# A perceiver layer on one core: the order of a program's branch arms, and the last products, sums and stores in halves

## The chip, the cores and the metric

The kernel runs on one core of a Trainium2 chip. The metric is the device time of the program in microseconds. Before the change three runs gave 994.02, 991.90 and 992.71, a median of 992.71. One more execution was recorded by the profiler; it took 989.35 us, and from its first to its last instruction 987.6 us.

TensorE (PE) multiplies, VectorE (DVE) and ScalarE (ACT) work on its results, GpSimd (POOL) computes and issues gathers, and SyncE (SP) issues most DMAs. Each engine has its own stream of instructions and its own sequencer, which handles waits, branches and the issue of DMAs. When a program branches, every engine has to branch.

## The reference

The input `x` is [1, 256, 512], the context [1, 4096, 512], all in float32. One layer is computed:

- cross attention of 256 queries with 16 heads of 128 (4 heads for keys and values) over the 4096 context rows and the layer's own rows (these causally), with RMS norm and rotary positions on queries and keys;
- a state-space block (projection, causal convolution, scan in chunks of 128, gate, projection);
- a mixture of experts. With `xn` the normalized state of a row:

```python
scores = sigmoid(xn @ gate_w)                 # 32 experts
w, e   = top_k(scores, 6); w = w / (sum(w) + 1e-20)
routed = sum_k w[k] * (silu(xn @ wg[e[k]]) * (xn @ wu[e[k]])) @ wd[e[k]]
shared = (silu(xn @ sg) * (xn @ su)) @ sd
out    = x + routed + shared
```

An expert's hidden size is 192, that of the shared expert 384. Each stage adds to the residual state, which the kernel keeps in `x_sb`, two tiles of 128 rows by 512 columns; what `x_sb` holds at the end is the output.

## The kernel before, in words

**Two branches.** Whether attention may use a fixed bound on its scores is computed from the norm weights on the chip (`small_scores`, line 110) and loaded into a register of every engine as `flag` (line 1601). At line 1602 the program branches: one arm is `layer(lctx, True)`, with bounded attention, the other (line 1605) is `layer(lctx, False)`. Both arms are written out in full. The data given take the bounded arm. The second branch stands near the end of the layer, at line 1572: `crowded` says whether some expert got more rows than its place holds, and is loaded as `some` (line 1557). The data given take the arm without crowding. It holds the last additions and the stores; the other arm runs all experts over again and comes after it in the program. At the end of the arm of line 1572 that is written first, an engine jumps over the code that follows: the crowded arm and the general layer.

**The experts.** Experts are worked on in 16 pairs (`NP`), one a round `n`. A round does the gate and up products (`gate_up`, or `gate_up_halves` where an expert of the pair has room for 64 rows), turns the hidden values, and does the down product of the round before. Rows come from `xg` by gather; results go to `ye` by a store on ACT's queue, and are gathered again by row (`gather`, line 1322, six rows per token, on POOL) and added with their weights on DVE (`add`, line 1330). The last three pairs (`n` from `LAST` = 13) don't pass through `ye`: `spread_last` brings their hidden values to token order with a product (lines 1424 and 1425) and `down_into` (line 1457) sums their down products for both row tiles in two PSUM banks, `total[0]` and `total[1]`. A float32 product is two passes of TensorE, each with its own weight load, so `down_into` of one tile has three products and six passes.

**The order at the end.** In the last round, `n` = 15, TensorE does `down_into` of pair 14 for tile 0, the spreading of pair 15, and `down_into` of pair 14 for tile 1; between them DVE adds the gathered rows of tile 1. After the loop `down_into` of pair 15 follows, tile 0 and then tile 1. In the arm without crowding, `finish(t)` (line 1567) adds `total[t]` to `x_sb` on DVE and `store(t)` (line 1570) issues the store on SP, once for each tile.

**Buffers touched.** `ps_x` is a pool of two PSUM banks with the tag `x`, used for the transposes of gathered rows (line 1370); the last of these belongs to pair 15. `total` comes from `ps_ye`.

**What closes the program.** After the joins, every engine comes to the program's end, which the profile puts down to line 1650: SP waits for the semaphores of all queues and engines, every engine drains and signals, and all meet twice. At the start, SP issues the first loads (lines 94 to 104) ahead of its branch and those of `wk`, `wq` and `wv` (line 189) behind it; TensorE's first product (line 218) stands behind the branch.

## Time and profile before

| | us |
|---|---|
| median of three runs (lowest, highest) | 992.71 (991.90, 994.02) |
| the profiled execution | 989.35 |
| its span, first to last instruction | 987.6 |
| TensorE busy | 968.4 |
| DVE busy | 497.8 |
| ACT busy | 386.5 |
| POOL busy | 206.0 |
| TensorE busy in the first 25 us | 19.60 |
| end of TensorE's last pass, by the chain | 979.71 |
| last addition on DVE, start and length | 979.74, 0.69 |
| the two stores, start of issue | 977.95, 980.46 |

"Busy" counts the instructions of an engine's datapath, not branches, waits or the issue of DMAs. The chain of work that ended last is followed back from the last such instruction, so what comes after it has no part in it. A line that ends in q (SPq, DVEq, PEldq) is of an engine's sequencer. In the list for one source line, a row gives the operation, how often it ran, its least, median and greatest duration in ns, and the start of the first and of the last one in us. The queues called "instruction" bring instructions to the engines.

### The profile page before, as it was taken

How to read it: one execution, taken by the hardware profiler on the slowest of the kernel's cores; microseconds unless marked ns; L12 is line 12 of the kernel's file. 1: busy time of each engine (PE TensorE's matmuls, PEld its weight loads, DVE VectorE, ACT ScalarE, POOL GpSimd, SP SyncE). 2: the span in 40 equal slices, each digit the busy share in tenths (PEclk: the TensorE clock that was granted, in tenths of full speed). 3: DMA queues.
4: the chain of work that ended last, by engine and by line, in shares of the span. 5: the costliest groups of instructions: out<-in, count | busy, mean ns of one | idle time of the engine just before them, and what ended most of it. 6: DMA issues, size and time to landing. Idle time of an engine off the chain costs nothing.

```text
span 987.6 us, 8901 instructions
## 1 busy us (share of the span) xinstructions
PE 968.4 (98%) x2742; PEld 456.0 (46%) x2742; DVE 497.8 (50%) x999; ACT 386.5 (39%) x851; POOL 206.0 (21%) x212
## 2 busy tenths in 40 slices
PE   7999999999999999999999999999999999999996
PEld 3444444444444444444444444444465655555442
DVE  4456555454453544544535545458496766422134
ACT  3645444443443434434434444353253731222210
POOL 4443001001100200200200100000013224554533
PEclk9999999999999999999999999999999999999999
DMA  9734142222313304304204112240046452999953
GB/s 319 235 74 118 56 117 94 45 39 111 85 21 128 85 2 147 82 4 150 66 20 124 56 35 46 83 128 1 0 157 199 184 193 106 353 351 352 397 221 117
DMA packets 131580, 125.91 MB, mean 127 GB/s; under 512 B 80225, under 2 KB 99586, under 8 KB 126274
## 3 DMA queue, kind: packets, MB, share of 16 engines
q1 hardware_dynamic: 119216, 77.96, 26.2%
q0 software_dynamic: 7984, 41.16, 11.2%
q10 hardware_dynamic: 4322, 6.11, 1.7%
q8 instruction: 24, 0.39, 0.2%
q14 instruction: 34, 0.28, 0.1%
HBM read 89.02 MB, written 36.19 MB: 127 GB/s over the span
## 4 chain that ended last, share of the span: by engine, by line
PE 94%; DMA 2%; DVE 1%; ACT 1%; POOL 1%; issue 1%; SPq 0%; POOLq 0%; DVEq 0%
PE scT L567 23%; PE oT L592 23%; PE ps_kv L364 17%; PE ps_egu L218 5%; PE ps_self L218 3%; PE ps_v L218 2%; PE ps_o L790 2%; PE ps_ye L1466 2%; PE ps_xbc L218 1%; PE ps_out L984 1%; PE ps_egu L1389 1%; PE ps_k L218 1%; PE ps_sgu L218 1%; PE total L1457 1%; PE xgTp L1370 1%; PE ps_ye L1469 1%
## 5 line engine op out<-in xcount | busy, mean ns | idle before, releaser
L583 DVE TENSOR_TENSOR lacc<-lacc,prT 128x512 f32<-128x512 f32 x256 | 182.6, 714 | 239.2 <-ACT prT L573 238.5
L573 ACT ACTIVATE prT<-scT,bq,rk 128x512 f32<-128x512 f32 x256 | 198.9, 777 | 253.9 <-PE scT L567 241.8
L567 PE MATMUL scT<-qT,kT 128*128 128x512 f32 x536 | 271.7, 593 | 0.0
L592 PE MATMUL oT<-prT,v 128*128 128x512 f32 x528 | 268.3, 592 | 0.0
L567 PEld LDWEIGHTS scT<-qT,kT 128*128 128x128 f32 x536 | 101.1, 190 | 124.8 <-issue 121.9
L592 PEld LDWEIGHTS oT<-prT,v 128*128 128x128 f32 x528 | 100.2, 190 | 125.8 <-issue 115.8
L196 POOL TENSOR_TENSOR rk<-pv,mhalf 128x4 f32<-128x4 f32 x32 | 32.3, 1010 | 369.2 <-DVE pv L195 369.2
L364 PE MATMUL ps_kv<-wkv,fast 128*128 128x512 f32 x112 | 53.4, 592 | 0.0
L254 ACT ACTIVATE sq<-kraw 128x128 f32<-128x128 f32 x128 | 35.6, 278 | 45.2 <-DVE kraw L382 43.2
L364 PE MATMUL ps_kv<-wkv,ctx 128*128 128x512 f32 x112 | 52.8, 592 | 0.0
L364 PE MATMUL ps_kv<-fast,fast 128*128 128x512 f32 x112 | 52.6, 592 | 0.0
L598 DVE TENSOR_TENSOR oacc<-oT,oacc 128x512 f32<-128x512 f32 x64 | 43.6, 681 | 0.0
L364 PEld LDWEIGHTS ps_kv<-wkv,fast 128*128 128x128 f32 x112 | 21.3, 190 | 26.8 <-issue 26.8
L364 PEld LDWEIGHTS ps_kv<-fast,fast 128*128 128x128 f32 x112 | 21.3, 190 | 26.8 <-issue 21.8
L364 PEld LDWEIGHTS ps_kv<-wkv,ctx 128*128 128x128 f32 x112 | 21.3, 190 | 26.8 <-issue 23.7
L358 POOL TENSOR_TENSOR fast<-ctx 128x512 f32<-128x512 f32 x7 | 9.4, 1337 | 113.1 <-PE ps_kv L364 94.2
L382 DVE TENSOR_TENSOR kraw<-ps_kv,fast 128x256 f32<-128x256 f32 x42 | 17.9, 426 | 28.2 <-PE ps_kv L364 28.2
L1441 DVE TENSOR_TENSOR hid<-si,ps_egu 128x128 f32<-128x128 f32 x18 | 5.2, 287 | 51.2 <-ACT si L1439 51.2
L790 PE MATMUL ps_o<-wo,qT 128*128 128x512 f32 x64 | 28.8, 592 | 0.0
L218 PE MATMUL ps_self<-wq,xT 128*128 128x512 f32 x64 | 28.1, 592 | 0.0
L603 DVE RECIPROCAL lacc<-ps_l 128x512 f32<-128x512 f32 x8 | 26.8, 3348 | 0.1
L364 PE MATMUL ps_kv<-fast,ctx 128*128 128x512 f32 x56 | 26.3, 592 | 0.0
(392 smaller groups left out, 1129.3 us busy)
## 6 DMA issues: line engine op xcount, KB each, us to landing
xg<-xn SPq DMA_DIRECT2D x6, 2560.0 KB, 9.7
ctx<-in_ctxT_dram SPq DMA_DIRECT2D x7, 1024.0 KB, 5.0
kd<-tr SPq DMA_DIRECT2D x112, 64.0 KB, 2.2
kT<-kd SPq DMA_DIRECT2D x28, 256.0 KB, 2.9
ye<-y_sb ACTq DMA_DIRECT2D x22, 256.0 KB, 8.4
wq<-in_wq_dram SPq DMA_DIRECT2D x4, 1024.0 KB, 14.2
wo<-in_wo_dram SPq DMA_DIRECT2D x4, 1024.0 KB, 7.7
w_in<-in_W_inT_dram SPq DMA_DIRECT2D x4, 1024.0 KB, 5.8
```

The costliest lines, as they stand in the source:

```text
L196: return G.tensor_tensor(dst, v[:, :n], mhalf[:, :n], ALU.pow)
L218: TE.matmul(ps, lhs(k), rhs_of(k), start=(k == 0), stop=(k == KD - 1))
L254: S.activation(sq[:, h, :], raw[:, h, :], AF.Square, accum_out=ss[:, h:h + 1])
L364: TE.matmul(ps, lhs(k), rhs(k), start=(start and k == 0), stop=(k == 1), skip_group_check=True)
L567: scored.append(TE.matmul(sc, kT[:, g, i * P:(i + 1) * P], qT[:, t, heads4(g), :].rearrange("p h q -> p (h q)"), start=True, stop=True).ins)
L573: S.activation(pr, sc, AF.Exp, bias=shift, scale=SCALE if r is None else r[:, i, g:g + 1])
L583: V.tensor_tensor(la, la, pr, ALU.add)
L592: TE.matmul(outs[g, t], v[:, i, g * HD:(g + 1) * HD], pr, start=(n == 0), stop=last)
L598: V.tensor_tensor(ov, outs.pop((g, t)), ov, ALU.add)
L603: V.reciprocal(rl, ps)
L790: TE.matmul(m["ps_o", t], aT[:, t, h, :], wo[j][:, h % 4, :], start=(h == 0), stop=(h == NH - 1))
L1466: TE.matmul(ps[i], h[:, i, :], wd[i], start=True, stop=False)
```

## The change

There are four edits.

1. The arms of both branches change places: the test becomes `some == 1` with the crowded arm first, and `flag == 0` with the general layer first. The arms that the given data take are now the last in the program.
2. The additions `finish` move in front of the branch on `crowded`, out of both arms. In the common arm only stores are left.
3. `total[1]` no longer takes in pair 15: its sum ends with pair 14 and is added to `x_sb` at once. The product of pair 15 for tile 1 is done in two halves of 256 columns, each in a bank of its own from `ps_x` (`part`), and each half is added by itself.
4. The store of tile 1 is issued in two halves of columns.

```diff
-            def down_into(self, n, total, first, last, tiles=range(NT)):
+            def down_into(self, n, total, first, last, tiles=range(NT), cols=slice(0, DM)):
...
-                        TE.matmul(total[t], h[:, j, t * P:(t + 1) * P], wd[j],
+                        TE.matmul(total[t], h[:, j, t * P:(t + 1) * P], wd[j][:, cols],
...
-                        main.down_into(n - 1, total, False, False, [1])
+                        main.down_into(n - 1, total, False, True, [1])
...
-            main.down_into(NP - 1, total, False, True)
-
-            def finish(t):
-                V.tensor_tensor(x_sb[:, t, :], total[t], x_sb[:, t, :], ALU.add)
-
-            def store(t):
-                nc.sync.dma_start(out[t * P:(t + 1) * P, :], x_sb[:, t, :])
-
-            with tc.If(some == 0) as arms:
-                for t in range(NT):
-                    finish(t)
-                    store(t)
-            with arms.Else():
-                for t in range(NT):
-                    finish(t)
+            halves = [slice(i * DM // 2, (i + 1) * DM // 2) for i in range(2)]
+            parts = [main.ps_x.tile([P, DM // 2], FP, tag="x", name="part") for _ in halves]
+
+            def finish(t, ps, cols=slice(0, DM)):
+                V.tensor_tensor(x_sb[:, t, cols], ps, x_sb[:, t, cols], ALU.add)
+
+            def store(t, cols=slice(0, DM)):
+                nc.sync.dma_start(out[t * P:(t + 1) * P, cols], x_sb[:, t, cols])
+
+            main.down_into(NP - 1, total, False, True, [0])
+            finish(1, total[1])
+            for cols, part in zip(halves, parts):
+                main.down_into(NP - 1, {1: part}, True, True, [1], cols)
+            finish(0, total[0])
+            for cols, part in zip(halves, parts):
+                finish(1, part, cols)
+
+            with tc.If(some == 1) as arms:
                 main.weights = {}
...
                     store(t)
+            with arms.Else():
+                store(0)
+                for cols in halves:
+                    store(1, cols)
...
-    with tc.If(flag == 1) as arms:
+
+    with tc.If(flag == 0) as arms:
+        with ExitStack() as lctx:
+            layer(lctx, False)
+    with arms.Else():
         with ExitStack() as lctx:
             layer(lctx, True)
-    with arms.Else():
-        with ExitStack() as lctx:
-            layer(lctx, False)
```

## The prediction

> **What bounds the kernel now.** I read the page first, then the end of the chain that ended last, then the two lines of code at which the program branches and joins, then the DMAs of the last 9 us, then the start.

> ```profile
> PE 968.4 (98%) x2742; PEld 456.0 (46%) x2742; DVE 497.8 (50%) x999; ACT 386.5 (39%) x851; POOL 206.0 (21%) x212
> ```

> TensorE is busy for 98% of the span, so only the places where it isn't can give much. The windowed view shows 19.60 us of TensorE work in the first 25.00 us and none in 980 to 988. The chain's last pieces (start, length, what):

> ```profile
> 971.97 7.74 PE total L1457 x18
> 979.71 0.02 issue
> 979.74 0.69 DVE x_sb L1567
> ```

> The arithmetic is over at 980.43, but the span is 987.62. These 7.2 us have no row in the chain: they belong to branches, waits and one store. The line of the branch on `crowded` and the program's closing line show them (first and last start in us):

> ```profile
> L1572 SPq COMPARE_BRANCH  x2: 38/40/43, 846.4 to 981.3; - x2
> L1572 POOLq COMPARE_BRANCH  x2: 34/38/41, 965.3 to 977.6; - x2
> L1572 ACTq COMPARE_BRANCH  x2: 34/36/38, 971.8 to 972.0; - x2
> L1572 PEldq COMPARE_BRANCH  x2: 63/1754/3444, 973.7 to 979.9; - x2
> L1572 DVEq COMPARE_BRANCH  x2: 51/53/55, 976.2 to 979.7; - x2
> ```

> ```profile
> L1650 POOLq DRAIN  x3: 40/107/6594, 980.2 to 987.4; - x3
> L1650 ACTq DRAIN  x2: 8/44/81, 975.0 to 987.1; - x2
> L1650 DVEq DRAIN  x2: 10/34/58, 983.0 to 987.1; - x2
> L1650 PEldq DRAIN  x2: 8/40/73, 983.4 to 987.1; - x2
> ```

> Each engine branches twice: into the common arm, and out of it over the code of the crowded arm. The first costs nothing (it falls through). After the second, the next instruction comes at 975.02 on ACT (3.05 us later), 980.19 on POOL (2.57), 982.95 on DVE (3.20), 983.39 on PE (3.50); SP leaves at 981.26 and goes on at 983.92 (2.66), by the trace's single records. Between lie the fetches of instructions:

> ```profile
> q14 instruction: 6, 0.05, 1.9%
> q8 instruction: 2, 0.03, 1.7%
> ```

> These are the instruction queues from 979 to 988: eight fetches in 9 us, where the page has 58 in the whole span. SP's fetch starts 0.93 us after its branch and takes 0.53; the next block is asked for at 984.48, and SP, which has done seven of twelve closing waits by 984.36, does the eighth only at 986.01: a second stall of 1.65 us[...]. SP then ends its waits and sends its last signal at 986.41; all engines meet, and the span ends 1.21 us later.

> ```profile
> L1570 SPq DMA_DIRECT2D out_dram<-x_sb x2: 338/338/338, 978.0 to 980.5; - x2
> DMA to landing us min/median/max: 2.1/2.5/3.0
> ```

> The last store landed at 983.42 (980.46 + 2.96), before SP came out of its jump. So the end is set by SP's two fetch stalls, not by the store.

> [...] the records here show 16 KiB on q8 but 8 KiB on q14. [...] Here a hardware-queue store took 2.12 us undisturbed and 2.96 beside the fetches. [...]

> **The change, part by part.** Sums are made on the profiled execution: span 987.62, its own time 989.35, 3.36 below the median of 992.71 (so the comparison carries an offset; I apply the difference to the median).

> *Common arm of `crowded` last.* Each engine now takes the branch on entering. SP does so at about 846.4 and has nothing to do until 977.9: 2.66 us behind 131 us of waiting, free. POOL at 965.3 has six gathers queued until 973.3, then waits: free. ACT at 971.8 has no more work: free. PE at 973.7 has 14 passes (6.0 us) queued; a jump of 3.50 ends at 977.2: free, and if the sequencer reached it 2.5 us later still free. At the end all fall through: −2.66 and −1.65 us for SP. DVE is the exception. Its flag load (0.33 us) and branch follow its last addition, because the sequencer stands at that addition until TensorE is done: start 979.74, branch 0.40 us after the load's start (975.75 to 976.15 now), so 980.15; plus 3.20 gives 983.35. With the smallest jump seen (2.57) 982.72, with the largest (3.50) 983.65.

> *Last products by halves.* Three weight blocks in two passes are six passes of 0.429 us at 512 columns; now twelve at 256. The row at L1425 (256 columns) has 0.320 us between its two passes and 0.216 to the next product. The first follows a switch of the array from 64 to 128 rows; here there is none, so I take 0.215: 12 x 0.215 = 2.58, as before. The upper bound 12 x 0.320 = 3.84 would end TensorE 1.26 us later; below nothing it can't go, the columns are the same. Weight loads double, but a load starts 0.11 us after the previous one in the transposes, less than 0.215. The `part` banks come from `ps_x`, last read at 958.8: no wait.

> *Additions.* `finish(1)` on `total[1]` follows the gathers' last addition (ends 976.46) and takes 0.69: 977.15, when `total[0]` is just complete (977.14): nothing on the path. `finish(0)` ends at 977.9 as before. The first half ends near 978.9 under TensorE's second half. The last addition has 256 columns: the same form at L382 takes 0.426 us against 0.692: −0.27.

> *Stores.* Three issues of 0.338 us; the last waits only for the last half: 980.18. Landing 2.12 to 2.96 later: 982.3 to 983.1. SP's remaining waits, 0.07 each, at most six behind it, and two signals: 982.5 to 983.7.

> *Common arm of the whole layer last.* Now every engine jumps at the start (3.41 to 3.52 us, SP 7.61). ACT is back at 6.5 and needed at 11.80; DVE 6.7, needed 11.06; POOL 6.0, needed 12.83. TensorE:

> ```profile
> 2.20 7.22 DMA wkv<-in_wk_ctx_dram
> 9.46 9.35 PE ps_k L218 x20
> ```

> It is back at 3.49 + 3.50 = 6.99 instead of 5.29, has four passes (1.72) to do before the weights of 9.41, and later stands another 0.5 us until 11.67 for a context block. So it may return as late as 8.24 for nothing; beyond that each us costs one. SP's loads from L189 on move from 7.71 to 10.4. What is issued before (3.8 MB) keeps the DMA engines busy until about 14.2 (the DMA view's rates sum to 3.7 MB in the first 14.0 us), and `wk` lands at 18.33 but is used at 23.39. Even a shift by 5 us is covered: nothing.

> *Sum.* SP's path now ends at 982.5 to 983.7, DVE's at 983.35. I take DVE's: 983.35 + 1.21 = 984.56, against 987.62: −3.06. 992.71 − 3.06 = 989.65.

> **Rivals.**
> (a) *Half of it is eaten* (0.18): POOL's DRAIN of 6.59 us may be real work; starting at 977.7, after its INC_SWDGE_SEM of 1.77, it ends at 984.3, and the span at 985.1: −2.5. [...] Or passes of 0.320 us: −1.8. About 991.0. For it: the DRAIN ends 0.37 us after SP's signal, longer than a signal needs; against: its record starts when the engine begins to stand.
> (b) *The joins still jump* (0.07): if the blocks aren't laid out in the order of the arms, SP keeps 2.66 + 1.65, and only 0.27 is gained: 992.4.
> (c) *Slower* (0.06): TensorE's refill at the start. Five engines fetch while the DMA engines are 72 to 100% busy; past 8.24 us each us is paid 1:1. It cancels the gain when TensorE is back at 11.3 and is measurably slower from 13.3: a jump of 9.8 us for 3.50 seen. At that it gives 994.7 and more. Against: the fetch at 35.8, on as busy engines, took 1.15 us against 0.98.
> (d) *More* (0.07): DVE's jump is hidden because its flag is read earlier; then SP at 982.5 sets the end at 983.7: −3.9, or with shifts elsewhere −5: 988.3.

> **How the numbers follow.** The main case has 0.62, with its own range 988.7 to 990.7 (jump 2.57 to 3.50 us, runs that differ by about 1 us). From (a) it reaches 991.6, from (d) 987.7; with the three runs' own scatter (991.9 to 994.0) I take 987.5 to 991.9, leaving out (b) and (c). A measurement can tell about 0.2% (2.0 us) from no change, so faster is below 990.7: 0.62 nearly whole, 0.07, a little of (a): 0.71. Same: the rest of (a) and (b): 0.23. Slower: 0.06.

> **What would show it.** The span near 984.6; last TensorE pass ending near 979.7; DVE's last addition of 256 columns near 979.74; a branch on DVE near 980.15 and its DRAIN near 983.3 as the last signal; no stall in SP's closing waits; three stores, the last at 980.2; TensorE's first matmul near 7.0 instead of 5.29 and the chain of 9.46 unmoved. Wrong it would be if TensorE's work at 9.46 or the first gather (956.60) has moved, if the closing waits still contain a gap above 1 us, or if POOL's DRAIN keeps its 6.6 us and ends last.

## The result

The changed kernel takes 994.83 us (median of 13 runs, 993.49 to 996.12) against 992.03 us before (13 runs, 990.79 to 995.08). The ratio is 1.0024, with a 95% interval from 1.0015 to 1.0034: slower by about 2.8 us, where 3.1 us less was forecast (989.65 from 992.71). The profiled execution took 994.73 us, its span is 993.0. TensorE's work is the same, its share is smaller:

```profile
PE 967.6 (97%) x2748; PEld 457.5 (46%) x2748; DVE 497.6 (50%) x1001; ACT 386.6 (39%) x851; POOL 205.7 (21%) x212
```

**The start.** The list of the branch on `flag`, now at line 1612 (least, median, greatest duration in ns, then the starts in us):

```profile
L1612 POOLq COMPARE_BRANCH  x1: 45/45/45, 3.5 to 3.5; - x1
L1612 PEldq COMPARE_BRANCH  x1: 8472/8472/8472, 3.6 to 3.6; - x1
L1612 DVEq COMPARE_BRANCH  x1: 67/67/67, 3.6 to 3.6; - x1
L1612 SPq COMPARE_BRANCH  x1: 45/45/45, 7.7 to 7.7; - x1
```

TensorE's branch alone shows its jump as its own duration: 8.47 us, where 3.50 was assumed. By the single records POOL goes on at 9.69 and SP at 12.76. DVE's next instruction, at 12.16, doesn't show its jump: it is a wait for the load of `x_sb`, which ends just then. The view of `x_sb` has this as DVE's wait (us, times):

```profile
  DMA x_sb<-in_x_dram: 9.3, 1
```

The instruction fetches begin at 8.06, 9.16, 9.29 (8 KB each) and 9.65 (16 KB), one more at 11.19, and take 0.3 to 1.04 us. The one of 16 KB, on q8, is taken for TensorE's: 6.1 us lie between its branch and the start of the transfer, 1.0 in the transfer, and 1.4 between its end and the end of the branch. At TensorE's jumps at the end, too, a fetch of 16 KB ends 1.4 us ahead of the end of the branch (981.95 and 983.34 in the kernel before), or 1.3 (985.29 and 986.62 in the changed one). So it is not the transfer that is long, but what lies ahead of it. The chain then reads:

```profile
4.74 7.37 DMA ctx<-in_ctxT_dram
12.12 0.10 issue
12.22 12.36 PE ps_k L218 x24
24.58 0.87 PE lnT L212 x8
```

The piece of 7.37 us is put down to a context load, but it is TensorE that isn't there; its first product starts at 12.22 for 5.29. And 24 passes take 12.36 us, 0.515 each, though a pass at full pace takes 0.429. TensorE's busy time (in each line the figure ahead of the first bracket, behind the stretch and its length) shows both places that matter; the first line is the kernel before, the other two the changed one:

```profile
0.00:25.00 25.00, 19.60 (x51) 8.65 (x52) 10.82 (x28) 8.97 (x31) 11.76 (x18) 1.00 0.90 320
0.00:25.00 25.00, 12.78 (x30) 5.91 (x31) 8.35 (x25) 5.95 (x20) 9.46 (x15) 1.00 0.90 310
980.00:988.00 8.00, 7.60 (x24) 4.18 (x22) 5.21 (x9) 0.00 (x0) 1.09 (x1) 1.00 0.41 124
```

In the first 25 us it is 12.78 us, 6.8 less than before. The first product behind the context, `lnT`, starts at 24.58; before it was 18.81 (9.46 + 9.35). That is 5.77 us, and it divides so: the block of passes begins 2.76 later (12.22 for 9.46), it holds the four passes that were done ahead of 9.46 before (1.72), and the rest, 1.29, is slower pace: 24 passes exceed 0.429 each by 2.06, the 20 of before by 0.77.

**The end.** The chain's last pieces, and the program's closing line, now 1660:

```profile
979.86 5.15 PE total L1457 x12
985.01 2.60 PE part L1457 x12
987.61 0.02 issue
987.64 0.42 DVE x_sb L1570
```

```profile
L1660 POOLq DRAIN  x3: 40/107/6531, 985.6 to 992.7; - x3
L1660 SPq DRAIN  x3: 7/7/7, 991.3 to 992.4; - x3
...
L1660 DVEq DRAIN  x2: 10/14/17, 991.2 to 992.5; - x2
```

Twelve passes of 256 columns take 2.60 us, and the last addition starts at 987.64. To the end of the span there are 5.37 us more, where the kernel before had 7.88 (979.74 to 987.62): the end did gain, by 2.5 us. But the last to arrive is POOL: its drain of 6.53 us runs from 985.64 to 992.17, 0.8 us longer than SP's (991.37) and 1.0 longer than DVE's (991.17). SP's one remaining gap is no fetch, by SP's waits:

```profile
SPq L1660 <- DMA out_dram<-x_sb: 1.3, 1, 1.3
```

**The middle.** Near 850 us TensorE falls back by another 2.2 us against the first profile of before: ACT's first activation of the expert rounds (line 1439) starts at 855.33, 3 us after the products that it reads (before, it started at 846.4). Whether this belongs to the change is a question for the runs.

### The profile page after: what moved, and what is told of

The parts are those of the page before. It is cut to its first block, busy times and chain, and to the rows that moved or that the text cites. A ratio compares the mean times of both kernels' runs of the same rounds, so it can differ in the third digit from the quotient of the medians.

```text
span 993.0 us, 8913 instructions
## 1 busy us (share of the span) xinstructions
PE 967.6 (97%) x2748; PEld 457.5 (46%) x2748; DVE 497.6 (50%) x1001; ACT 386.6 (39%) x851; POOL 205.7 (21%) x212
## 4 chain that ended last, share of the span: by engine, by line
PE 92%; DMA 3%; DVE 2%; ACT 1%; issue 1%; POOL 1%; POOLq 0%; DVEq 0%; ACTq 0%
PE oT L592 23%; PE scT L567 23%; PE ps_kv L364 17%; PE ps_egu L218 5%; PE ps_self L218 3%; PE ps_v L218 2%; PE ps_o L790 2%; PE ps_k L218 2%; PE ps_ye L1466 2%; PE ps_xbc L218 1%; PE ps_out L984 1%; DMA ctx<-in_ctxT_dram 1%; DMA xg_sb<-xg,place 1%; PE ps_sgu L218 1%; PE ps_ye L1469 1%
## 5 line engine op out<-in xcount | busy, mean ns | idle before, releaser
L382 DVE TENSOR_TENSOR kraw<-ps_kv,fast 128x256 f32<-128x256 f32 x42 | 17.9, 425 | 28.2 <-PE ps_kv L364 28.2
L218 PE MATMUL ps_self<-wq,xT 128*128 128x512 f32 x64 | 28.1, 592 | 0.0
L218 PE MATMUL ps_k<-wkv,ctx 128*128 128x512 f32 x32 | 16.0, 657 | 12.2 <-DMA ctx<-in_ctxT_dram 12.2
```

The costliest lines, as they stand in the source:

```text
L218: TE.matmul(ps, lhs(k), rhs_of(k), start=(k == 0), stop=(k == KD - 1))
```

## The experiments

All ratios are to the kernel before on the same chip; an interval is at 95%.

**One branch at a time.** In the first kernel only the branch on `crowded` is turned, with additions ahead of it and halves (the whole-layer branch stays in its old order):

```diff
-    with tc.If(flag == 0) as arms:
+    with tc.If(flag == 1) as arms:
         with ExitStack() as lctx:
-            layer(lctx, False)
+            layer(lctx, True)
     with arms.Else():
         with ExitStack() as lctx:
-            layer(lctx, True)
+            layer(lctx, False)
```

> The changed kernel with the whole-layer branch as before (bounded arm first), all else as changed. Theory A (the loss is the engines' jump at the program's start, where instruction fetches wait behind queued loads, and, in the profile, one ACT fetch at 855 us that only the new place of the code causes): TensorE's first product is back near 5.3 us, ACT has no gap at 855, and only the end's gain is left: 2.55 us below before, 989.5, ratio 0.9974. Rival B (additions ahead of the branch and the half products cost time in the middle or at the end): no faster than before, ratio 1.000 or more. Rival C (code moved about costs wherever it is): somewhere in between, with another late engine.

It took 993.58 us, ratio 1.0009 (1.0000 to 1.0018). TensorE's first product is back at 5.18, so the loss at the start belongs to the whole-layer branch. But there is no gain at the end: from the last addition to the end of the span it is 8.48 us, more than before. Its lists of the branch on `crowded` and of the closing line:

```profile
L1583 DVEq COMPARE_BRANCH  x2: 47/60/73, 983.6 to 987.4; - x2
```

```profile
L1660 POOLq DRAIN  x3: 40/107/6594, 983.7 to 991.4; - x3
...
L1660 DVEq DRAIN  x2: 10/40/70, 990.8 to 991.1; - x2
```

DVE jumps twice one after the other: over the crowded arm (983.60 to 987.34) and, once there, over the general layer (987.43 to 990.77). With the crowded arm behind the common one, a single jump passes over both: in the kernel before DVE went on 3.20 us after its branch.

The second kernel is the kernel before with only the whole-layer branch turned (the same lines the other way round).

> The kernel before with only the whole-layer branch turned (general layer first). Theory A: TensorE's first product at 12.2 us for 5.3, DVE, POOL and SP back 6 to 9 us after their branch, and the ACT gap near 846 if it belongs to the place of the code; the joins at the end cost what they did, so 5.3 us above before (what the changed kernel lost, 2.8, and the 2.55 gained at its end): 997.4, ratio 1.0054; without the ACT gap 1.003 to 1.004. Rival B: no change at the start, ratio 1.000.

It took 994.77 us, ratio 1.0023 (1.0016 to 1.0030): the whole loss of the change, no more. The expectation was wrong by 3 us, and the trace says why. The start is lost as in the changed kernel, but the end is gained as well:

```profile
11.79 13.39 PE ps_k L218 x24
25.18 0.87 PE lnT L212 x8
```

```profile
L1650 POOLq DRAIN  x3: 40/107/6531, 986.2 to 993.4; - x3
```

From the last addition to the end it is 5.70 us. POOL still jumps over the crowded arm, but goes on 0.16 us after its branch (986.09 to 986.25), where a jump over the general layer as well took 2.57. So turning the whole-layer branch is the change as far as time goes: it moves one jump over a whole layer from the end to the start. All the other edits together, the turn at `crowded` and the halves, shorten the end by another 0.3 us in the profile (5.37 for 5.70) and bring nothing that the medians show.

The third has both branches in their old order, but additions ahead and halves:

```diff
-            with tc.If(some == 1) as arms:
+            with tc.If(some == 0) as arms:
+                store(0)
+                for cols in halves:
+                    store(1, cols)
+            with arms.Else():
                 main.weights = {}
...
-            with arms.Else():
-                store(0)
-                for cols in halves:
-                    store(1, cols)
...
-    with tc.If(flag == 0) as arms:
+    with tc.If(flag == 1) as arms:
```

> The kernel before with both branches in their old order, but additions ahead of the branch, last products and stores by halves. Theory A: the half addition saves 0.27 us, the end is still set by SP's jump over the crowded arm behind its last store (two stalls of 2.66 and 1.65): ratio 0.9997, no change to be measured. Rival B (halves are what the end gained): 2.5 us less, ratio 0.9975. Rival D (twelve passes of 256 columns and three stores cost more than six and two): 0.5 to 1.5 us more, ratio 1.0005 to 1.0015.

992.82 us, ratio 0.9996 (0.9990 to 1.0003), as expected, but the end isn't SP's:

```profile
L1660 POOLq DRAIN  x3: 40/107/6593, 983.6 to 990.8; - x3
L1660 SPq DRAIN  x3: 7/7/7, 990.1 to 990.5; - x3
```

POOL's drain ends at 990.24, SP's last signal is at 990.12, with a second stall of 2.1 us in it.

**What makes the jump long.** All eight early loads of SP go behind the branch:

```diff
-    load_ctx0(0, 1)
-    load_wkc(0, 1)
-    load_wkc(1, 1)
-    load_wkc(2, 2)
-    nc.sync.dma_start(x_sb, a["x"].rearrange("(t p) d -> p t d", p=P))
-    load_ctx0(1, 1)
-    load_ctx0(2, 2)
-    nc.sync.dma_start(wvc, a["wv_ctx"].rearrange("(k p) n -> p k n", p=P))
...
+        load_ctx0(0, 1)
+        load_wkc(0, 1)
...
         wk = wpiece(a["wk"], "wk")
```

> The changed kernel, but all eight loads that SP issues ahead of the whole-layer branch (3.8 MB) are issued behind it. Only small loads on ACT's queue are then under way when the engines jump. Theory A (instruction fetches wait behind the queued loads): the jump of PE, DVE and POOL at the start falls from 8.5, 8.6 and 6.1 us to about 3.5, as at the quiet end, so that they are back near 7; the loads come later by SP's own jump (back near 7), so the first product is not before 10 us all the same. Rival E (a jump at the start is dear by itself: five engines fetch at once, cold memory): still 6 to 8.5 us.

```profile
L1612 PEldq COMPARE_BRANCH  x1: 4052/4052/4052, 3.5 to 3.5; - x1
L1612 DVEq COMPARE_BRANCH  x1: 67/67/67, 3.5 to 3.5; - x1
L1612 SPq COMPARE_BRANCH  x1: 45/45/45, 3.7 to 3.7; - x1
```

TensorE's jump falls from 8.47 to 4.05 us: all first fetches now begin between 5.12 and 5.22, 1.4 to 1.7 us after the branches. DVE and SP are back only at 8.57 and 8.48, 5.1 and 4.8 us after theirs; that part of the expectation missed. All transfers of 8 KB had ended by 5.58, so here some 3 us lie behind the transfer, and no record says what fills them. In all it takes 998.68 us (one run), since the loads start late.

With only the last three loads (by the sizes of the eight, 1.8 of 3.7 MB) moved, in the same way:

> The changed kernel with the last three of SP's eight early loads (context rows 128 to 511 and the value weights, 1.8 of 3.8 MB) issued behind the whole-layer branch. Theory A (fetches wait behind queued loads): TensorE's jump lies between the 4.1 us without loads and the 8.5 us with all of them, about 6 us, so its first product comes near 9.5 to 10; the second context block comes only after SP's own jump, so TensorE waits again after four passes, and in all the time stays within 1 us of the changed kernel (ratio to the kernel before 1.0015 to 1.0035). Rival E (the amount queued doesn't matter, only whether any large load is under way): the jump stays at 8.5 us.

```profile
L1612 PEldq COMPARE_BRANCH  x1: 7718/7718/7718, 3.5 to 3.5; - x1
```

994.47 us, ratio 1.0018 (1.0010 to 1.0026). The jump is hardly shorter, nearer to rival E's 8.5 us than to the 6 of theory A, and the fetches begin at 8.48 to 8.88. The amount queued in all doesn't set it. In both kernels the same five loads (1.8 MB) are issued before 3.5 us; the other three follow after the four branches, from 4.74 us on in the changed kernel and behind SP's own jump here. A fetch that waits behind what was queued ahead of it, and not behind what comes later, would fit TensorE's jump in all three kernels. It doesn't fit SP's: in the changed kernel SP branches at 7.66 behind all eight loads (3.7 MB) and is back at 12.76, when its queue has moved only 2.82 MB. So what is shown is that the loads under way at the branch make the jump long; the order in which fetches and loads are served stays open.

**The slow passes.** TensorE gets products on constants at its start, into a bank that nothing reads; seven of them (14 passes) first:

```diff
+    with tc.tile_pool(name="ps_warm", bufs=1, space=PSUM) as ps_warm:
+        cold = ps_warm.tile([P, 4, P], FP, tag="warm", name="cold")
+        for i in range(7):
+            TE.matmul(cold, ones, ones.unsqueeze(1).to_broadcast([P, 4, P]), start=(i == 0), stop=(i == 7 - 1))
     mhalf = const.tile([P, NH], FP, name="mhalf")
```

> The changed kernel with seven more products (14 passes of 512 columns on constants, into a bank that nothing reads) on TensorE ahead of the whole-layer branch. Theory A (besides the late fetch, TensorE pays its slow first passes, 0.85 to 1.0 us each for 0.43, a second time: before the change they ran while weights were on their way): the first four or five passes after 12.2 us come at 0.43 us, 1.9 us less than the changed kernel, about 992.9, ratio to the kernel before 1.0005. Rival F (the slow passes have another cause, such as waiting operands, or the added passes hold up the jump): no gain, ratio 1.0024 or more.

993.60 us, ratio 1.0008 (0.9998 to 1.0017), 1.6 thousandths less than the changed kernel.

```profile
11.74 12.23 PE ps_k L223 x24
```

The added passes themselves are slow five times (0.85 to 1.0 us apart), then 0.43. They end at 9.5, TensorE is back at 11.74, and its passes there are first 0.50 and 0.58 apart, then 0.85 again. In the windowed view, TensorE's busy time and then the granted clock:

```profile
12.80:15.30 2.50, 2.50 (x4) 0.50 1.00 338
```

The single clock records say the same: full from 5.69, half from 12.52, full again from 15.93. So the slow passes are a slow clock, and not waiting operands, as rival F had it. In this profile the 24 passes need hardly less than the 12.36 of the changed kernel, and the gain of the timed runs isn't seen in it. With eleven products:

> As e6_warm, but with eleven products (22 passes) ahead of the branch, so that TensorE works until it is back from the jump. In e6_warm the 14 passes ended at 9.5 us, TensorE stood for 2.2 us, and after two quick passes at 11.74 and 12.25 the next four came 0.85 us apart again. Theory A (the clock falls back when TensorE stands, and the slow passes cost some 2 us): all passes from about 12 us on come at 0.43 us; about 2 us less than the changed kernel, ratio to the kernel before 1.0003 (0.9995 to 1.0010). Rival F (the added passes hold up the branch or the first product): no better than e6_warm, 1.0008 or more.

```profile
1.21 12.06 PE cold L119 x22
13.27 10.30 PE ps_k L223 x24
```

993.24 us, ratio 1.0009 (1.0002 to 1.0015). Now the 24 passes take 10.30, 0.429 each. But the added ones keep TensorE until 13.27, though its jump ended at 12.29, and in all the expectation missed: the ratio is the one of rival F. So nine:

> As e9_warm_long, with nine products (18 passes) for eleven. In e9_warm_long the passes all came at 0.43 us, but the 22 added ones ended only at 13.27 us, about 1 us after TensorE was back from its jump (12.29). Eighteen end near 11.55. Theory A: first product near 12.0 to 12.2, all passes at 0.43 us; 2 us less than the changed kernel, ratio to the kernel before 1.0000 (0.9993 to 1.0008). Rival F (the gain is used up): like e9_warm_long and e6_warm, 1.0008 or more.

```profile
11.60 10.54 PE ps_k L223 x24
22.14 0.87 PE lnT L217 x8
```

992.49 us, ratio 1.0001 (0.9993 to 1.0009): 2.3 thousandths less than the changed kernel, as expected. `lnT` starts at 22.14 for 24.58; the pace of the 24 passes makes 1.8 us of this (10.54 for 12.36), an earlier first product 0.6. The second part is no work of the added products as far as is known: in this profile TensorE's jump ended at 11.44, in that of the changed kernel at 12.05. What is left of the late start is about what the end gains.

**A version that beats both.** The third kernel above, with the branches in their old order, and three such products (6 passes):

> The kernel of e3_halves_only (both branches in their old order) with three more products (6 passes of 512 columns on constants) on TensorE at its start. Theory A: the slow passes, 5 to 9 of them in the profiles so far, are over when the weights of 9.4 to 10.0 us land; 0.5 to 1.7 us less than the kernel before, 990.6 to 991.8, ratio 0.9983 to 0.9995. Rival F: no gain, ratio 0.9996 as without them, or a loss where the added passes delay the first products.

991.63 us, ratio 0.9987 (0.9978 to 0.9995). The passes on the weights come at 0.43 to 0.65 us from 10.10 on. This kernel keeps the jump at the end (8.16 us from the last addition to the end of the span). In its one profile `lnT` starts at 19.28, in the range of the kernels without added products (18.81 to 20.73); the verdict rests on the timed runs. They show it faster than the kernel before; against the kernel with halves alone, 0.9996 (0.9990 to 1.0003), the intervals overlap, so what the three products add is not clear of the noise.

**What ends last.** The changed kernel, with POOL kept busy behind its gathers:

```diff
                 for cols in halves:
                     store(1, cols)
+                for _ in range(28):
+                    G.memset(ones, 1.0)
```

> The changed kernel with 28 fills of a constant tile (0.2 us each) on POOL in the arm without crowding, behind its gathers. POOL comes to the closing part about 3 us later. Theory A (its long drain is real work of 6.5 us and ends last): the drain keeps 6.5 us and the span ends about 3 us later against the last addition. Rival G (the drain only stands until the others are done): it shrinks to about 3.5 us and the end stays where it was.

```profile
L1662 POOLq DRAIN  x3: 40/107/6531, 989.7 to 997.2; - x3
L1662 SPq DRAIN  x3: 7/7/7, 990.8 to 996.9; - x3
```

The drain starts at 989.74, 2.74 us after the last addition (987.00), where in the changed kernel it starts 2.00 ahead of it: 4.7 us later, more than the 3 expected. It still takes 6.531 us. Everything else is done by 990.85 and stands until 996.27. From the last addition to the end it is 10.4 us for 5.37 (999.14 us in all, one run). So the drain takes its own 6.5 us and doesn't stand for the other engines; what it does in them no record says.

**The kernel before once more.**

> The kernel before once more, unchanged, for a second profile: the first one took 989.35 us where the median of its runs is 992.3. Theory A (the first profile was a lucky execution: its slow passes at the start were over after five, and ACT's first activation of the expert rounds, at 846 us, followed TensorE at once): this one has seven to nine slow passes, ACT some 3 us late near 848, and takes 991.5 to 993. Rival H (the kernel before has neither delay, and both belong to the changed code): five slow passes again, no delay near 847, about 989.5 to 990.5.

It took 991.42 us, a little under the range expected.

```profile
9.71 9.42 PE ps_k L218 x20
19.12 0.88 PE lnT L212 x8
```

```profile
844.54 4.28 another core or an unknown queue
...
848.90 0.33 ACT si L1439
```

```profile
L1650 POOLq DRAIN  x3: 40/107/6593, 982.3 to 989.4; - x3
L1650 SPq DRAIN  x3: 7/7/7, 988.3 to 989.1; - x3
```

Five slow passes again, so there the first profile was no exception and the expectation missed; but ACT is some 2 us late near 849 although nothing was changed. So the delay in the middle is not the change's: every profile but the first one of before has it, 1.8 to 2.2 us on TensorE. Its cause stays open: the profile names TensorE's products, which were done 2 to 3 us before, or, as here, nothing it knows, and in the kernel with halves only no instruction fetch lies between 842.5 and 860.5. Against this profile the account nearly closes: `lnT` 5.46 us later (24.58 for 19.12), the end 2.68 us shorter (5.37 for 8.05 from the last addition), which makes +2.8 us, the difference of the medians. The two profiles themselves differ by 3.3 us; the other 0.5 lies between `lnT` and the last addition and isn't explained.

## Why the prediction was wrong

**The step that failed: "It is back at 3.49 + 3.50 = 6.99".** The price of a jump was read at the quiet end and used at the start, where 1.8 MB stood in the queues. There it took 8.47 us, and even with the loads away 4.05. The rule of the prediction, free until 8.24 and 1:1 beyond, then gives 12.12 − 8.24 = 3.9 us of loss; with the slower pace, 1.3, the half microsecond of cover that was put down to a context block (what is real of it, passes late by 0.12 and 0.11, is already in that pace), and the 0.1 from 12.12 to the first product, it is the 5.8 that the first profile of before shows; against the second it is 5.5.

**Rival (c) was the case.** Its argument against itself was the fault: a fetch at 35.8 "took 1.15 us against 0.98". That is how long the transfer took, and transfers were short here too (0.3 to 1.04 us). What counts is the time from the branch to the next instruction, most of it ahead of the transfer here (6.1 of TensorE's 8.47 us), and a fetch behind which no branch stands doesn't show it. The rival's own price, 994.7 us for a jump of 9.8, is close to what came at 8.5, because it left out the slow passes.

**Slow passes, unforeseen.** Passes came 0.85 to 1.0 us apart for 0.43, and there were five, six or nine of them in three kernels that are the same there (the kernel before, the one with halves alone, and the one with only the branch on `crowded` turned). The step to full clock came 3.6 to 6.2 us after the first pass where the passes follow one another without a pause (3.67 in the changed kernel, from 12.22 to 15.89), and with seven added products 2.2 us of standing were followed by a slow clock (half from 12.52). Before the change four of five, from 5.29 to 9.34, ran while weights were on their way (the wait for them ended at 9.41) and cost little; behind the late jump each is paid, 1.29 us more in the first profiles. The prediction counted passes at 0.43 there although the trace of before has the slow ones at 5.29 to 9.46; so the four passes that it priced at 1.72 us took about 4.

**"So the end is set by SP's two fetch stalls": wrong.** POOL's drain ended last in the kernel before too (986.78, SP's signal 986.41), as in every kernel here but the one with two jumps: 0.82 to 0.84 us lie between its end and that of the span (1.15 in the run that kept POOL busy). Rival (a) named it, and its argument for, that 0.37 us is longer than a signal needs, holds: POOL's signal of 986.92 ended SP's wait at 986.96. The argument against, that its record only starts when the engine begins to stand, fell with the run that kept POOL busy. The end's gain was forecast as 3.06 and measured as 2.5 to 2.7: its size is that of POOL's jump of 2.57, which falls away. SP's stalls fall away too, and had to, since SP's signal came only 0.37 us before the end of POOL's drain, but they don't set the size; why SP stalled a second time before, for 1.65 us, was not shown. The forecast was near by luck, for the wrong reason.

**Which edit gains.** The prediction gave the gain at the end to the arms of `crowded`. It belongs to the whole-layer branch, since the general layer is the code that costs POOL a long jump (2.57 us for 0.16). Alone, the turn at `crowded` made the kernel with halves slower, 1.0009 for 0.9996 or 0.8 us by the medians; 0.5 of it stands at the end of the two profiles (8.48 for 8.01 us from the last addition), where DVE's second jump comes behind the first.

**What held.** DVE's branch near 980.15, 0.41 after its last addition: measured 0.46 after it, with a jump of 2.96 for 3.20. Twelve passes of 256 columns in 2.58: measured 2.60. The last addition, 0.425 us: but its 0.27 is no gain, since POOL sets the end (ratio 0.9996). SP's loads 5 us later at no cost: they moved from 7.71 to 12.76, and after 12.22 the chain shows no wait for a transfer in the first 25 us.

**The first profile.** It took 989.35 us, 3 below the median, and I treated the offset as harmless. It hides one of the delays that other executions have; profile against profile would have told of 5.4 us for 2.8.

## What to carry to other kernels

The same jump cost TensorE 3.5 us at the quiet end, 4.05 at the start without loads and 8.47 with loads under way: price a taken branch at the place it will stand, by the time from branch to next instruction, not by the length of the fetch, and look first whether that next instruction waits for something else. Code that is not run has to be jumped over somewhere; moving it moves the jump. Here it cost nothing where an engine still had work queued or had something to wait for: TensorE's jump of 3.91 us at 982.71 in the changed kernel left no gap in its passes, and DVE's at the start ended no later than its wait for `x_sb`. At a program's end look for the engine whose closing work ends last, here GpSimd with its drain, before pricing the others, and at its start consider idle products for TensorE while it waits for weights: nine of them took back about 2 us of the changed kernel's loss.
